# Loading the weight pieces of the projections two pieces ahead of their split, in three slots

## The chip, the cores and the metric

The kernel runs on one core of one Trainium2 chip. The metric is the device time of one execution in microseconds (us), as a median over runs.

## The reference

Two batches of 2048 tokens with 2048 channels are normalised; the result goes through one head of attention (width 512) and through a gated low-rank branch, and both are added to the input.

```python
def attn(x, Wqkv, bqkv, Wo, bo):            # d = 512
    q, k, v = split3(einsum('bsc,cf->bsf', x, Wqkv) + bqkv)
    attn = softmax(einsum('bqd,bkd->bqk', q, k) / sqrt(d))
    return einsum('bqd,dc->bqc', einsum('bqk,bkd->bqd', attn, v), Wo) + bo

def ffn(x, A_w, B_w, Wq_w, keys):           # 64 experts of rank 8, top 16
    scores = einsum('bsr,er->bse', einsum('bsd,rd->bsr', x, Wq_w), keys)
    gate = softmax_of_top16_scattered(scores)
    z = einsum('bsd,nd->bsn', x, A_w)       # n = 64 * 8 = 512
    return einsum('bsn,on->bso', z * repeat(gate, 8), B_w) * 2

x = x + attn(layernorm(x), ...) + ffn(layernorm(x), ...)
```

## The kernel before

All products keep single-precision quality by splitting each operand into a high and a low half in the type `fp32r` and multiplying three times (`product`, line 135 of the profile: low by high, high by low, high by high). The high half is a copy on ScalarE (`split_hi`, line 127), the low half a subtraction on VectorE (`split_lo`, line 130).

The work has three parts. The projections take the first 1297 us: for eight blocks of 512 tokens they make queries, keys, values, the router's inputs and the low-rank features. The attention follows, then the output projection. Blocks are taken in pairs, and in the projections a pair's four quarter products (two token blocks by two halves of the channels, two halves of the features) are replaced by seven products of sums and differences, named `P1` to `P7`. The sums of weights are made once, during the first pair, on GpSimd (`four_sums`, lines 541 to 544) and stored in device memory (`sq_d`, `sv_d`), from where the later phases load them.

The weights come in **pieces** of 128 partitions by 1024 or 1056 elements (512 or 528 KB). `pieces` lists all 218 in the order of use:

- 12 pieces `F` (block 0, features), 8 pieces `Q` and `R` (block 1, values by half of the channels), 6 pieces `P3` and 24 pieces of `P6`, `P5`, `P7`, `P4` for the rest of the first pair;
- 56 pieces for each of the other three pairs: per phase six pieces of features and two of values (`V`).

`fetch(n)` loads piece `n` on SyncE's queue (SP, line 622) and splits it. The slots are:

- a loaded piece goes into the ring `r_pw` of three slots (tags G8, G9, G7); the `F` pieces of features 0 and 2 go into the rings `r_set`, since their weights are summed in place later;
- the halves go into `r_ph`, six slots, which is three pieces' worth.

The product of piece `n` is followed by `fetch(n + 2)`, so that two pieces' halves stand ready or are being made. `features`, `values_by_half`, `third` and `phase` are the four loops over pieces; each does for one piece the product, the fetch, `flush()` (the stores that are pending), the eviction, and then a few **steps** of other work: loads of the next tokens (`x_steps`, line 640, with their normalisation, lines 647 and 648), splits of the next moving operand (`split_steps`, tile `t`), sums of weights with their loads and stores (`set_load`, line 1149; `set_out`, line 1156; `part_load`, line 1169; `part_out`, line 1178), the router's top 16 (`choose`, lines 480 to 493), and, in the last pair, key and query steps (lines 1002 to 1128).

The kernel is written with a framework that traces the calls and lets a planner set the order on each engine's queue: an instruction takes a place when, in the plan, its inputs and its slot are there, and of several the one called first goes first. Semaphores follow from the order of the calls. `behind(...)` adds edges to this: what is called in the block is queued, on each engine, behind the last instruction recorded under the names given. The steps stand behind `"sp"`, and `last["sp"]` is the newest weight load.

Of the kernel before, what the change touches and what calls it, by code (L numbers as in the profile page):

```python
# [8 lines left out]
F32 = mybir.dt.float32  # L9
FR = mybir.dt.float32r  # L10
# [52 lines left out]
def attn_ffn_kernel(ctx: ExitStack, tc, x, xT, wq, wv, wob, bqk, bv, bo, keysT, out):  # L63
# [20 lines left out]
    def wide(*js):  # L84
        return Ring(sb, *(f"G{j}" for j in js))
# [40 lines left out]
    def split_hi(hi, src):  # L126
        return nc.scalar.copy(hi, src)  # L127

    def split_lo(lo, src, hi, eng=None):
        return (eng or nc.vector).tensor_tensor(lo, src, raw(hi), ALU.subtract)  # L130
# [61 lines left out]
    r_ph = wide(0, 1, 2, 3, 4, 5)  # L192
# [126 lines left out]
    def first_block(steps):  # L319
# [128 lines left out]
        for c2 in range(N2):  # L448
            w = wv_piece(1, c2)
            if c2 == N2 - 1:  # L450
                fetch(0)
            for t in range(NT):
                mul(ps[t], w, t, c2)
            with behind("sp", "pe", "dve"):
                for st in steps[c2 : c2 + 1] if c2 + 1 < N2 else steps[c2:]:
                    st()
        fetch(1)
        for t in range(NT):
            values_out(0, t, 1, r_ev, qr, ps[t])
# [95 lines left out]
    def value_sums(m):  # L555
# [33 lines left out]
    pieces = [  # L589
        (0, "F", 2 * p + f1, ch) for p in range(NFP // 2) for ch in range(2) for f1 in range(2)  # L590
    ]
# [8 lines left out]

    r_set = {0: big(*GROUPS[0]), 2: big(*T_SLOTS[8:])}

    def fetch(n):

        if n >= len(pieces):
            return
        j, ph, it, g = pieces[n]
        w = WHERE.get(ph)
        ring = r_pw
        if ph == "F":  # L610
            shape, src = [P, HC * P], wq[0, g][it]
            ring = r_set.get(it, r_pw)
        elif ph in ("Q", "R"):
            shape, src = [P, HC // 2, VH], wv[it, int(ph == "R")][:, 4 * g : 4 * g + 4, :]
        elif it == "V":
            shape = [P, HC // 2, VH]
            src = sv_d[w][g] if isinstance(w, int) else wv[w][:, 4 * g : 4 * g + 4, :]
        else:
            shape = [P, HC * P]
            src = sq_d[w][it] if isinstance(w, int) else wq[w][it]  # L620
        ws = ring(shape, F32, "pw")
        last["sp"] = nc.sync.dma_start(ws, src)
        if ph == "F" and it in r_set:
            held[it, 0, g] = ws
        hi, lo = (r_ph(shape, FR, "pw") for a in range(2))
        last["hi"] = split_hi(hi, ws)
        last["dve"] = split_lo(lo, ws, hi)
        ready[n] = hi, lo
# [178 lines left out]
    def phase(j, ph, n, more={}):  # L807
# [9 lines left out]
        for m, it in enumerate(items):  # L817
# [4 lines left out]
            for g in range(2 if it == "V" else 1):  # L822
                w = ready.pop(n)
                n += 1
                if it != "V":
                    for c in range(HC):
                        product(
                            ps, lambda a: w[a][:, c * P : (c + 1) * P],
                            lambda b: ops[c // 2][b][:, c % 2, :], c == 0, c == HC - 1,
                        )  # L830
                else:
                    for cc in range(HC // 2):
                        c = g * HC // 2 + cc
                        for t in range(NT):
                            sl = slice(t * P, (t + 1) * P)
                            product(
                                ps[t][:, :VH], lambda a: ops[c // 2][a][:, c % 2, sl],
                                lambda b: w[b][:, cc, :], c == 0, c == HC - 1,
                            )
                fetch(n + 1)  # L840
# [26 lines left out]
    def features():  # L867


        tiles, qT, wk, gx = {}, None, None, {}  # L870
        for k, (_, _, fp, ch) in enumerate(pieces[:12]):
            if ch == 0:
                tiles[fp] = acc()
            ps, w = tiles[fp], ready.pop(k)
            if fp >= 2 * 2 and ch == 0:
                gx[fp - 4] = gate(gfs[0], fp - 4)
            for c in range(HC):
                product(
                    ps, lambda a: w[a][:, c * P : (c + 1) * P], lambda b: xn[ch * HC + c][b],
                    c == 0 and ch == 0, c == HC - 1, ch == 1,  # L880
                )
            last["dve1"] = last["dve"]
            fetch(k + 2)
            flush()
            if ch == 0:
                if fp % 2 == 0:
                    XU[0, fp // 2] = r_xu([P, 2, T], F32, "xu")
                nc.scalar.copy(XU[0, fp // 2][:, fp % 2, :], ps)
            else:
                feature_out(0, ND * (fp // 2) + fp % 2, ps, gx)  # L890
            with behind("pe"):
                if k == 0:
                    qT = router(qr)
                if k == 1:
                    wk = choose(qT)
                if k == 4:
                    gfs[0] = gates(0, wk)
            with behind("sp", "pe", "dve1"):
                for st in beside_F.get(k, []):
                    st()  # L900
        return len(tiles) * 2

    def values_by_half(n):

        for ph in "QR":
            tiles = [tsp[0, ph, 0], tsp[0, ph, 1]]
            for h in range(2):
                ps = [acc() for t in range(NT)]
                for g in range(2):
                    w = ready.pop(n)  # L910
                    n += 1
                    for cc in range(HC // 2):
                        c = g * HC // 2 + cc
                        x_ = tsp[0, ph, c // 2]
                        for t in range(NT):
                            sl = slice(t * P, (t + 1) * P)
                            product(
                                ps[t][:, :VH], lambda a: x_[a][:, c % 2, sl],
                                lambda b: w[b][:, cc, :], c == 0, c == HC - 1,
                            )  # L920
                    last["dve1"] = last["dve"]
                    fetch(n + 1)
                    if g == 1:
                        flush()
                        values_half_out(ph, h, ps)
                        flush()
                    with behind("sp", "pe", "dve1"):
                        for st in beside_V.get((ph, h, g), []):
                            st()
        return n  # L930
# [20 lines left out]
    def third(n):  # L951

        r_w = big(25), big(27), big(28)
        for m, it in enumerate(MIXED):
            ps, w = acc(), ready.pop(n)
            n += 1
            for c in range(HC):
                product(
                    ps, lambda a: w[a][:, c * P : (c + 1) * P],
                    lambda b: tsp[0, "R", c // 2][b][:, c % 2, :], c == 0, c == HC - 1,  # L960
                )
            last["dve1"] = last["dve"]
            fetch(n + 1)
            flush()
            if it % 2 == 0:
                WU[it // 2] = r_w[it // 2]([P, 2, T], F32, "wu")
            nc.scalar.copy(WU[it // 2][:, it % 2, :], ps)
            with behind("sp", "pe", "dve1"):
                for st in beside_V.get(m, []):
                    st()  # L970
        return n
# [257 lines left out]
    n = features()  # L1229
    qr1 = const.tile([P, NT, 32], F32, name="qr1", bufs=1)  # L1230
    nc.gpsimd.memset(qr1, 0.0)
    n = values_by_half(n)
    r_t = big(*T_SLOTS[4:], *T_SLOTS[:4])
    n = third(n)
# [3 lines left out]
    n = phase(0, "P6", n, {0: [la], 1: [sa, one], 3: [oa], 4: [lb]})  # L1238
    n = phase(0, "P5", n, {0: [sb_], 2: [ob], 3: [lc]})
    n = phase(0, "P7", n, {0: [sc_], 2: [oc], 3: [ld]})  # L1240
    n = phase(0, "P4", n, {0: [sd_], 2: [od]})
    for j in PAIRS[1:]:
        for ph in PHASES:
# [5 lines left out]
            n = phase(j, ph, n)  # L1249
# [16 lines left out]
    r_ph = wide(0, 1, 2)  # L1266
# [477 lines left out]
    for g in range(begin[-1]):  # L1744
# [6 lines left out]
        j, n = divmod(g, NG1)  # L1751
# [131 lines left out]
```

## Time and profile before

| | |
|---|---|
| runs, us | 2580.57, 2581.15, 2585.92; median 2581.15 |
| span of the profiled execution, us | 2582.2 (the page gives no other time of this execution) |
| granted TensorE clock, mean | 0.998 |
| TensorE (PE) busy | 2556.8 us |
| VectorE (DVE), ScalarE (ACT), GpSimd (POOL) busy | 1981.2, 926.9, 560.8 us |
| DMA | 615.41 MB, mean 238 GB/s |
| weight pieces: ScalarE high half, `pw<-pw` | 218 of 1058 ns |
| weight pieces: VectorE low half, `pw<-pw` | 218 of 1324 ns |
| weight pieces: load, issue to landing | 3.2 / 3.8 / 8.7 us (least, median, most) |

PE is the matrix engine's multiplication and PEld its weight load. SPq marks an instruction of SyncE's queue, mostly the issue of a DMA. A timeline line has the start, the duration, the engine, the line of the kernel, the operation, output and input tiles, and in brackets how long the engine was idle before it and what ended that. A line of the view of waits has who waited for whom, the total in us, the number of times and the longest.

### The profile page before, as it was taken

What the parts mean: (1) busy time and instruction counts of PE and PEld (TensorE: products, weight loads), DVE (VectorE), ACT (ScalarE), POOL (GpSimd) and SP (SyncE); (2) the same over time, 40 slices, a digit from 0 to 9 for tenths busy, and PEclk for the clock granted to TensorE, in tenths of its full rate; (3) what the DMA queues carried; (4) which work ended last, traced back from release to release, by engine and by line L of the source; (5) the groups of instructions that cost most, each with busy time, mean ns of one, the idle gap of its engine ahead of it and who ended that gap; (6) DMA issues with size and microseconds to landing.
All of it is one profiled execution on the core that took longest, in us unless ns stands there. A gap on an engine that the chain in (4) does not pass through costs nothing. (4 is left out here: it accounts for less than half of the span.)

```text
span 2582.2 us, 34227 instructions
## 1 busy us (share of the span) xinstructions
PE 2556.8 (99%) x12546; PEld 2159.7 (84%) x12546; DVE 1981.2 (77%) x2692; ACT 926.9 (36%) x1327; POOL 560.8 (22%) x340
## 2 busy tenths in 40 slices
PE   9999999999999999999999999999999999999999
PEld 8897888888888889888887878878878888888887
DVE  7788997867778678777668768688597777797675
ACT  4333333232332323343345446354364222332221
POOL 2382310001000000000000000000013565576654
PEclk9999999999999999999999999999999999999999
DMA  8988964668356673678899798898897554665552
GB/s 297 311 300 276 354 224 144 227 212 274 125 176 225 211 250 120 201 269 270 315 310 309 240 338 278 282 324 290 277 320 265 182 162 157 203 200 179 167 168 101
DMA packets 334297, 615.41 MB, mean 238 GB/s; under 512 B 28409, under 2 KB 151345, under 8 KB 334129
## 3 DMA queue, kind: packets, MB, share of 16 engines
q1 hardware_dynamic: 318864, 583.33, 67.2%
q10 hardware_dynamic: 15264, 29.89, 3.3%
q8 instruction: 99, 1.62, 0.3%
q14 instruction: 70, 0.57, 0.1%
HBM read 457.76 MB, written 155.35 MB: 237 GB/s over the span
## 5 line engine op out<-in xcount | busy, mean ns | idle before, releaser
L135 PE MATMUL acc<-t,pw 128*128 128x512 f32 x3744 | 859.0, 390 | 6.4 <-DVE t L130 4.7
L135 PEld LDWEIGHTS acc<-t,pw 128*128 128x128 f32 x3744 | 699.8, 188 | 153.9 <-DVE t L130 6.4
L1629 PE MATMUL acc<-wb,s 128*128 128x512 f32 x2688 | 609.6, 389 | 0.0
L1629 PEld LDWEIGHTS acc<-wb,s 128*128 128x128 f32 x2688 | 504.4, 188 | 105.0 <-DVE s L130 0.2
L1613 POOL TENSOR_TENSOR xo<-xo,bo_bc 128x512 f32<-128x512 f32 x128 | 213.5, 1675 | 884.5 <-DMA bo_bc<-in_bo 592.3
L127 ACT CAST pw<-pw 128x1024 fp32r<-128x1024 f32 (+1 forms) x218 | 230.5, 1058 | 442.1 <-PE acc L135 287.8
L135 PE MATMUL acc<-ph,vt 128*128 128x512 f32 x1536 | 376.7, 390 | 0.3 <-ACT ot L1474 0.2
L130 DVE TENSOR_TENSOR pw<-pw 128x1024 fp32r<-128x1024 f32 (+1 forms) x218 | 288.7, 1324 | 95.9 <-ACT pw L127 94.3
L135 PEld LDWEIGHTS acc<-ph,vt 128*128 128x128 f32 x1536 | 287.7, 188 | 62.1 <-issue 1.2
L1335 PE MATMUL acc<-qt,kt 128*128 128x512 f32 x1344 | 333.9, 390 | 2.6 <-ACT sp L1345 1.5
L1335 PEld LDWEIGHTS acc<-qt,kt 128*128 128x128 f32 x1344 | 250.9, 188 | 58.9 <-DVE qt L130 2.2
L135 PE MATMUL acc<-pw,t 128*128 128x264 f32 x2400 | 295.9, 285 | 2.9 <-DVE pw L130 0.9
L135 PEld LDWEIGHTS acc<-pw,t 128*128 128x128 f32 x2400 | 294.2, 189 | 5.3 <-ACT pw L127 1.1
L127 ACT CAST s<-xz 128x1024 fp32r<-128x1024 f32 x112 | 118.0, 1054 | 375.1 <-PE acc L1629 300.3
L130 DVE TENSOR_TENSOR s<-xz,s 128x1024 fp32r<-128x1024 f32 x112 | 177.8, 1589 | 41.0 <-ACT s L127 41.0
L130 DVE TENSOR_TENSOR t<-xq,t 128x1024 fp32r<-128x1024 f32 x108 | 141.9, 1321 | 24.3 <-ACT t L127 24.1
L535 POOL TENSOR_TENSOR zt<-zt,g 128x512 f32<-128x512 f32 x28 | 44.6, 1603 | 516.0 <-DMA g<-gd 274.6
L127 ACT CAST t<-xq 128x1024 fp32r<-128x1024 f32 x108 | 113.1, 1051 | 114.1 <-DVE xq L667 59.6
L1618 DVE TENSOR_TENSOR xo<-xo,acc 128x512 f32<-128x512 f32 x128 | 86.9, 680 | 52.1 <-POOL xo L1659 25.2
L127 ACT CAST ph<-sp 128x512 fp32r<-128x512 f32 x128 | 79.4, 620 | 109.4 <-PE acc L135 108.5
L1654 POOL TENSOR_TENSOR xo<-xo,u 128x512 f32<-128x512 f32 x64 | 111.5, 1772 | 21.5 <-DVE u L1652 21.4
L225 DVE BATCH_NORM_STATS2 st<-xs 128x6 f32<-128x512 f32 x128 | 85.0, 683 | 39.5 <-DMA xs<-in_x 39.2
(174 smaller groups left out, 2229.4 us busy)
## 6 DMA issues: line engine op xcount, KB each, us to landing
vt<-v_d SPq DMA_DIRECT2D x128, 512.0 KB, 5.4
kt<-kp_d SPq DMA_DIRECT2D x224, 256.0 KB, 5.7
pw<-sq_d SPq DMA_DIRECT2D x96, 512.0 KB, 4.3
pw<-in_wq SPq DMA_DIRECT2D x72, 512.0 KB, 3.7
xo<-in_x SPq DMA_DIRECT2D x128, 256.0 KB, 3.0
xz<-oz_d SPq DMA_DIRECT2D x64, 512.0 KB, 4.4
out_y<-xo SPq DMA_DIRECT2D x128, 256.0 KB, 2.6
xq<-in_xT SPq DMA_DIRECT2D x56, 512.0 KB, 5.1
```

Of the source, the lines that this page charges most:

```text
L127: return nc.scalar.copy(hi, src)
L130: return (eng or nc.vector).tensor_tensor(lo, src, raw(hi), ALU.subtract)
L135: last["pe"] = nc.tensor.matmul(ps, st(a_), mv(b_), start=first and n == 0, stop=end and n == 2, skip_group_check=more,)
L225: nc.vector.bn_stats(st[:, parts, :], xt[:, h * 512 : (h + 1) * 512])
L535: nc.gpsimd.tensor_tensor(zt, zt, gx[n], ALU.mult)
L1335: last["pe"] = nc.tensor.matmul(ps, st[:, d, a, :], mv[c][:, d, :], start=not more and d == 0 and i == 0, stop=d == 1 and i == 2, skip_gro ...
L1613: nc.gpsimd.tensor_tensor(xs, xs, bo_bc[q // (NB // 2 * NH), c], ALU.add)
L1618: nc.vector.tensor_tensor(xs, xs, ps, op)
L1629: nc.tensor.matmul(ps, st[a_][:, kk, sl], mv[b_], start=not more and kk == 0 and n == 0, stop=kk == ND - 1 and n == 2, skip_group_check=more,)
L1654: nc.gpsimd.tensor_tensor(xo[q, t, a, 1], xo[q, t, a, 1], v, ALU.add)
```

## The change

`fetch` is divided. `load_piece(n)` takes the slot and issues the load of piece `n`, once; `fetch(n)` now calls it for `n` and for `n + 1` before it splits piece `n`. The slots, the number of loads and of splits, and the places where `fetch` is called stay as they are.

```diff
+    loaded = {}
+
+    def load_piece(n):
+
+        if n >= len(pieces) or n in loaded:
+            return
...
-        ws = ring(shape, F32, "pw")
+        ws = loaded[n] = ring(shape, F32, "pw")
         last["sp"] = nc.sync.dma_start(ws, src)
         if ph == "F" and it in r_set:
             held[it, 0, g] = ws
-        hi, lo = (r_ph(shape, FR, "pw") for a in range(2))
+
+    def fetch(n):
+
+        if n >= len(pieces):
+            return
+        load_piece(n)
+        load_piece(n + 1)
+        ws = loaded[n]
+        hi, lo = (r_ph(ws.shape, FR, "pw") for a in range(2))
         last["hi"] = split_hi(hi, ws)
         last["dve"] = split_lo(lo, ws, hi)
         ready[n] = hi, lo
```

More of the change, by code (lines that the diff above doesn't have):

```diff
@@ L601, in attn_ffn_kernel @@
     r_set = {0: big(*GROUPS[0]), 2: big(*T_SLOTS[8:])}
-    def fetch(n):
-        if n >= len(pieces):
+    loaded = {}
+    def load_piece(n):
+        if n >= len(pieces) or n in loaded:
             return
```

## The prediction

> **What bounds the kernel now.** I read the page's busy shares first, then PE's waits, then the timelines round each of them.
>
> The page's first lines:
>
> ```profile
> span 2582.2 us, 34227 instructions
> ...
> PE 2556.8 (99%) x12546; PEld 2159.7 (84%) x12546; DVE 1981.2 (77%) x2692; ACT 926.9 (36%) x1327; POOL 560.8 (22%) x340
> ```
>
> PE works for all but 2582.2 - 2556.8 = 25.4 us. The change adds and removes no matmul, so 25.4 us is all that any reordering could win, and only the part that lies in the projections (up to about 1297 us) is in its reach. The view of waits for PE, window 140 to 1300 us (total, times, longest):
>
> ```profile
> PE acc L135 <- DVE t L130: 5.3, 5, 2.4
> PE acc L135 <- DVE pw L130: 2.6, 2, 1.7
> PE acc L135 <- ACT pw L127: 0.9, 1, 0.9
> PE acc L135 <- ACT yv L941: 0.5, 1, 0.5
> ```
>
> Together 9.3 us. Only 3.5 us (2.6 + 0.9) name a weight piece (`pw`); 5.3 us name the moving operand `t`. PE's timeline shows where the larger ones are:
>
> ```profile
> 170.89 8.99 PE L135 MATMUL acc<-pw,t 128*128 128x264 f32 x72 [0.66 <-DVE t L130]
> 204.32 19.60 PE L135 MATMUL acc<-t,pw 128*128 128x512 f32 x85 [1.72 <-DVE pw L130]
> 226.32 1.65 PE L135 MATMUL acc<-t,pw 128*128 128x512 f32 x6 [2.40 <-DVE t L130]
> 228.59 6.87 PE L135 MATMUL acc<-t,pw 128*128 128x512 f32 x29 [0.61 <-DVE t L130]
> 1288.31 0.39 PE L135 MATMUL acc<-pw,t 128*128 128x264 f32 x1 [0.90 <-ACT pw L127]
> 1289.60 7.54 PE L135 MATMUL acc<-pw,t 128*128 128x264 f32 x47 [0.90 <-DVE pw L130]
> ```
>
> **Where a load really stands.** The code calls a load just before its split. The queue does not keep to that. One piece in the steady part, timeline round 726 us:
>
> ```profile
> 725.15 1.05 ACT L127 CAST pw<-pw 128x1024 fp32r<-128x1024 f32 x1 [0.21 <-PE acc L135]
> 726.24 1.23 DVE L130 TENSOR_TENSOR pw<-pw 128x1024 fp32r<-128x1024 f32 x1 [0.63 <-ACT pw L127]
> 727.49 0.33 SPq L622 DMA_DIRECT2D pw<-in_wq  x1
> ```
>
> The low half ends at 726.24 + 1.23 = 727.47, and a load is issued 0.02 us later: the split has just freed one of three slots, and the load that takes it is that of the piece three further on. Its own split comes some 14 us later, and a load lands in 3.8 us (median of the tile's view). The planner has moved the load as far ahead as three slots allow, one step further than the change asks. Counting loads and splits through the trace, most of the 206 pieces from the 13th on go like this. There the change can move nothing: 0 us: some 10 us lie between landing and split, and a load that lost one product of 5.5 us would still be in time.
>
> The exceptions are two crowded stretches of SP's queue, 115 to 205 us (weight sums) and 1196 to 1281 us (key and query steps). There a load is issued up to 15 us after its slot is free, in the order in which the code calls it, and its split waits for it:
>
> ```profile
> 188.45 1.05 ACT L127 CAST pw<-pw 128x1024 fp32r<-128x1024 f32 x1 [4.15 <-DMA pw<-sq_d]
> 194.89 1.05 ACT L127 CAST pw<-pw 128x1024 fp32r<-128x1024 f32 x1 [1.62 <-DMA pw<-sq_d]
> ...
> 1272.80 0.42 SPq L622 DMA_DIRECT2D pw<-in_wv  x1
> 1280.33 0.49 SPq L622 DMA_DIRECT2D pw<-in_wv  x1
> 1287.18 1.07 ACT L127 CAST pw<-pw 128x1056 fp32r<-128x1056 f32 x1 [8.21 <-DMA pw<-in_wv]
> ```
>
> **The change, part by part.** No instruction, byte or slot is added. Each load is called one piece earlier, so in a crowded stretch it takes about the place of the load before it.
>
> *The last piece (1280.33).* It takes the place of the one at 1272.80, 7.5 us sooner. It landed at about 1287.1 (6.8 us after issue), so now at about 1279.6; high and low half (1.07 + 1.26 us) are done by 1282 to 1283, before PE wants them at 1287.4. Both waits of 0.90 us go: -1.80 us. Nothing else is late there, since `kt` and `qt` loads are queued behind this load already.
>
> *The piece at 204.32.* Its load moves from 188.10 to the place of 185.36 or before, 2.7 us or more, and the high half (194.89, 1.62 us after ACT fell idle for the landing) moves with it. The low half, at 203.05, did not wait for it: it stood on DVE behind the top-k work of `choose` (197.6 to 203). Whether it gets ahead of that is up to the planner: 0 to -1.72 us. I take -1.72, since its high half is ready before that work starts; the 0 stays in the range.
>
> *The operand waits (`t`, 5.3 us).* These splits have no load in them. I take 0; the gain rival below prices them.
>
> *What is queued behind.* `behind("sp", ...)` puts a product's other steps behind the newest load, which is now one piece further and can start only when the split three before it is done. The trace shows that this binds early on:
>
> ```profile
> 67.94 0.34 SPq L622 DMA_DIRECT2D pw<-in_wq  x1
> 68.34 2.58 SPq L1149 DMA_DIRECT2D wu<-in_wq  x2
> ...
> 78.21 2.78 DVE L130 TENSOR_TENSOR pw<-pw 128x1024 fp32r<-128x1024 f32 x1 [6.34 <-ACT pw L127]
> ...
> 117.14 2.00 ACT L127 CAST t<-xq 128x1024 fp32r<-128x1024 f32 x2
> ...
> 122.30 2.35 DVE L130 TENSOR_TENSOR t<-xq,t 128x1024 fp32r<-128x1024 f32 x2
> ```
>
> `set_load(2)` (`wu`) left directly behind piece 7's load. Now it stands behind piece 8's, whose slot is freed by the split that ends at 78.21 + 2.78 = 80.99: 13 us later. What waits for it is POOL's sums, whose last waited until 100.99 for another split anyway: covered. The next place is `set_out(2)`, stores at 111.25 to 117.1. It now stands behind piece 12's load, whose slot is freed at 116.7 (DVE low half at 115.49, 1.21 us). That is 5.5 us for the first store, about 2 for the last. These stores free the slots of the first `Q` splits of `t` (117.14 on ACT, 122.30 on DVE). With 4 us to land, DVE's pair moves to about 125, 2.7 us later. The DVE chain behind it ended at 134.0, and the product that needs it starts at 137.0: 3.0 us of cover, so 0. If the shift persists to the `t` split at 170.85, which is already 0.66 us late, it costs up to 2.7. Against that DVE waits 9.1 us for high halves of `pw` between 140 and 215 (two waits, the tile's view), and these shrink. I take 0 and keep 0 to +2.7.
>
> [...]
>
> **Sum.** -1.80 - 1.72 = -3.5 us. The profiled execution's span, 2582.2 us (the page gives no other time of its own), becomes 2578.7. It stands 1.05 us above the runs' median of 2581.15, so on the median the forecast is 2577.6. Its own range: nothing from the piece at 204 and +2.7 from `t` give 2582.1; another 2 us from `t` waits give 2575.6.
>
> **The rivals.** About 0.2% (5.2 us) is what a measurement of this kernel can tell from no change: below 2576.0 is faster, above 2586.3 slower.
>
> *DVE catches up (faster).* If the 9.1 us in which DVE waited for high halves go, DVE comes earlier to its `t` splits, and the 2.40 + 0.61 us at 226 to 229 vanish with the 3.5: 2574.6. With everything in the projections gone, 9.3 us: 2571.8. For it: DVE is 83% busy from 140 to 235 us (78.92 of 95), so a few us of slack matter. Against: the split before 226.32 also stands among statistics that wait for `xs` loads. 0.27.
>
> *The steps queued behind a later load delay DVE (slower).* The place is 111 to 230 us: the stores of `set_out(2)` wait for a slot, then `t`, then DVE, in order. The small shift of 2.7 us, passed on to 170.9 and again to 226, both without slack, costs 5.4; less the 1.80 won at the end that is 2584.8, still "same". The whole 5.5 us of the first store passed on to both places costs 11.0, less 3.0 of cover and the 1.80: 6.2, or 2587.4. With another 2.7 at the piece of 204, 8.9: 2590. It decides once DVE's chain slips by more than the 3.0 us of cover at 137 and again behind it. For it: DVE is nearly without pause from 83 to 139. Against: the loads that DVE waits for come earlier in the same stretch. 0.28.
>
> *Nothing happens.* The queue already has all loads as early as slots allow, and the crowded ones are reordered without effect: 2581 to 2582. This is inside "same" with the forecast.
>
> **How the numbers follow.** The forecast has 0.30 and "nothing happens" 0.15, together 0.45 for the same; DVE catching up 0.27, DVE delayed 0.28. The range 2572 to 2590 goes from all projection waits gone to the price of the slower rival; I leave out about 0.04 below and 0.15 above, since a planned order that shifts can lose more than it can win.
>
> **What would show it.** Right: the two waits at 1288 gone, the last `pw` load some 7 us earlier; loads at 188 to 200 us earlier, ACT's waits of 4.15 and 1.62 us smaller; in the steady part a load still 0.0 us after the low half that frees its slot; PE's waits from 140 to 1300 us about 6 us in all instead of 9.3. Wrong: PE waiting for `t` between 137 and 230 us for longer than 5 us, `wu` loads not moved from 68 to 81, or new PE waits in the attention part.

## The result, and the profile after

The changed kernel takes 2587.93 us (median of 14 runs, 2583.05 to 2591.39) where the kernel before, run beside it, takes 2583.03 (14 runs, 2580.17 to 2585.98): ratio 1.0018, interval 1.0012 to 1.0025. It is 4.9 us slower, small but clear of no change. A second comparison (experiment 18) gave 2587.26 against 2582.33, ratio 1.0018 (1.0009 to 1.0027). The forecast was 2577.6. The one profiled execution of experiment 13 ran at a granted clock of 0.76 and is left out of everything below.

The page of the changed kernel begins:

```profile
span 2586.9 us, 34208 instructions
...
PE 2559.1 (99%) x12546; PEld 2162.5 (84%) x12546; DVE 1983.2 (77%) x2692; ACT 928.8 (36%) x1327; POOL 564.4 (22%) x340
```

The span is 4.7 us longer. PE does the same 12546 matmuls in 2.3 us more (2559.1 against 2556.8) and is idle for 2.4 us more (27.8 against 25.4). So two things are to be explained: longer waits, and matmuls that run slower. The view of waits for PE, 140 to 1300 us (total, times, longest), and PE's timeline where they are:

```profile
PE acc L135 <- DVE t L130: 5.7, 2, 5.1
PE acc L135 <- DVE pw L130: 5.7, 2, 4.3
```

```profile
170.19 9.00 PE L135 MATMUL acc<-pw,t 128*128 128x264 f32 x72 [0.60 <-DVE t L130]
200.82 19.29 PE L135 MATMUL acc<-t,pw 128*128 128x512 f32 x72 [4.33 <-DVE pw L130]
221.47 16.62 PE L135 MATMUL acc<-t,pw 128*128 128x512 f32 x72 [1.35 <-DVE pw L130]
268.14 20.64 PE L135 MATMUL acc<-t,pw 128*128 128x512 f32 x83 [5.10 <-DVE t L130]
...
1303.08 7.14 PE L1345 MATMUL acc<-qt,kt 128*128 128x512 f32 x30 [0.65 <-DVE vs L302]
```

In all 11.4 us instead of 9.3, and in other places: 4.33 and 1.35 at 200 and 221 us for weight pieces (1.72 before), nothing at 226 (3.01 before), 5.10 at 268 (1.45 before), nothing at 1288 (1.80 before). Following the start of the same matmul through both executions (times of the kernel before), the changed kernel is 0.7 us ahead at 194 us, 7.8 behind at 267, 7.3 behind at 1200, 4.4 behind at 1315 and 4.7 behind at the end. The whole loss is made between 194 and 268 us, in the first pair; 900 us of projections behind it change by half a microsecond, and some 3 us come back behind 1280.

**Slower matmuls.** The windows view (stretch, its length, then each engine's busy time and count, the granted clock, DMA share, GB/s) of the stretches behind the two long waits:

```profile
199.70:206.50 6.80, 5.68 (x13) 4.46 (x14) 6.80 (x30) 2.45 (x6) 3.49 (x2) 0.50 0.71 247
206.50:209.90 3.40, 3.40 (x16) 2.78 (x15) 3.40 (x7) 0.61 (x2) 0.00 (x0) 1.00 0.95 282
...
268.00:271.40 3.40, 3.26 (x8) 2.58 (x9) 3.40 (x5) 0.00 (x0) 0.00 (x0) 0.50 0.02 8
271.40:274.80 3.40, 3.40 (x17) 2.76 (x16) 3.28 (x6) 1.05 (x1) 0.00 (x0) 1.00 0.58 166
```

Behind each long wait PE is granted half its clock (0.50), for 6.8 and for 3.4 us: 8 matmuls where the next stretch has 17. Experiments 7 and 8 ask what that costs.

**Where the first pair went wrong.** The load that the prediction followed, `set_load(2)` (`wu`), is where it was foreseen, behind the ninth load of a piece:

```profile
67.82 0.34 SPq L624 DMA_DIRECT2D pw<-in_wq  x1
...
79.22 0.34 SPq L624 DMA_DIRECT2D pw<-in_wq  x1
...
80.08 0.90 SPq L1159 DMA_DIRECT2D wu<-in_wq  x2
```

It left at 68.34 before. What was not foreseen is what it does to POOL. The last of the sums that need it, in POOL's and DVE's timelines, before:

```profile
100.99 4.40 POOL L544 TENSOR_TENSOR pw<-pw 128x1024 f32<-128x1024 f32 x1 [11.10 <-DVE pw L130]
...
101.92 1.21 DVE L130 TENSOR_TENSOR pw<-pw 128x1024 fp32r<-128x1024 f32 x1
106.30 1.43 DVE L130 TENSOR_TENSOR pw<-pw 128x1024 fp32r<-128x1024 f32 x1 [3.17 <-ACT pw L127]
```

and after:

```profile
104.76 15.75 POOL L544 TENSOR_TENSOR pw<-pw 128x1024 f32<-128x1024 f32 x1 [7.30 <-DVE pw L130]
...
105.69 2.35 DVE L130 TENSOR_TENSOR pw<-pw 128x1024 fp32r<-128x1024 f32 x2
107.96 2.35 DVE L657 TENSOR_TENSOR xq<-xq,mb 128x1024 f32<-128x1024 f32 x2
110.23 2.35 DVE L658 TENSOR_TENSOR xq<-xq,mb 128x1024 f32<-128x1024 f32 x2
112.50 1.22 DVE L130 TENSOR_TENSOR pw<-pw 128x1024 fp32r<-128x1024 f32 x1
113.63 2.35 DVE L657 TENSOR_TENSOR xq<-xq,mb 128x1024 f32<-128x1024 f32 x2
115.90 2.35 DVE L658 TENSOR_TENSOR xq<-xq,mb 128x1024 f32<-128x1024 f32 x2
118.36 3.24 DVE L130 TENSOR_TENSOR pw<-pw 128x1024 fp32r<-128x1024 f32 x1
```

Each time the sum ends 2.26 us after DVE's first pause: before, DVE stops at 101.92 + 1.21 = 103.13 and the sum ends at 105.39; after, DVE works without a gap until 115.90 + 2.35 = 118.25 and the sum ends at 120.51. One sum, begun 3.8 us later, ends 15.1 us later, and in between DVE had no pause. In ten profiled executions (the kernel before, the changed kernel, experiments 1 to 7 and 18) the sum ends 2.25 to 2.28 us after the end of the unbroken run of DVE's in which it began, be it of 2 instructions or of 12; in experiment 12 it ran after the first instruction of such a run, before the next, and took 3.23 us. All sums of weights stand behind it on POOL: the first `part_sums` start at 120.5 instead of 105.4, the last at 197.1 instead of 184.9. Their loads and stores share SP's queue with the weight pieces, and so the piece for 200 us is late, not early:

```profile
189.48 2.27 SPq L1179 DMA_DIRECT2D hs<-in_wq  x4
191.79 0.43 SPq L624 DMA_DIRECT2D pw<-sq_d  x1
...
198.26 1.04 ACT L127 CAST pw<-pw 128x1024 fp32r<-128x1024 f32 x1 [2.33 <-DMA pw<-sq_d]
...
199.11 0.43 DVE L302 TENSOR_TENSOR vs<-acc,yv 128x264 f32<-128x264 f32 x1 [4.27 <-DMA v_d<-vs]
199.46 1.31 DVE L130 TENSOR_TENSOR pw<-pw 128x1024 fp32r<-128x1024 f32 x1
```

This piece (the third of the mixed pass `P3`) was issued at 185.36 before; now four loads of the sum chain (`hs`) are in front of it. It has landed when its high half starts, at 198.26, and PE waits until its low half is done.

### The profile page after: what moved, and what is told of

The parts are those of the page before. It is cut to its first block, busy times and chain, and to the rows that moved or that the text cites. A ratio compares the mean times of both kernels' runs of the same rounds, so it can differ in the third digit from the quotient of the medians.

```text
span 2586.9 us, 34208 instructions
## 1 busy us (share of the span) xinstructions
PE 2559.1 (99%) x12546; PEld 2162.5 (84%) x12546; DVE 1983.2 (77%) x2692; ACT 928.8 (36%) x1327; POOL 564.4 (22%) x340
## 3 DMA queue, kind: packets, MB, share of 16 engines
q8 instruction: 99, 1.62, 0.3%
## 5 line engine op out<-in xcount | busy, mean ns | idle before, releaser
L1623 POOL TENSOR_TENSOR xo<-xo,bo_bc 128x512 f32<-128x512 f32 x128 | 207.6, 1629 | 886.8 <-DMA bo_bc<-in_bo 587.1
L130 DVE TENSOR_TENSOR s<-xz,s 128x1024 fp32r<-128x1024 f32 x112 | 170.5, 1523 | 46.4 <-ACT s L127 46.4
```

Of the source, the lines that this page charges most:

```text
L1623: nc.gpsimd.tensor_tensor(xs, xs, bo_bc[q // (NB // 2 * NH), c], ALU.add)
```

## The experiments

Two theories stood at the start. **T1, the pins:** the steps that `behind("sp")` puts behind the newest load now wait for a later slot; that delays the sum chain. **T2, the call order:** the loads called earlier stand in front of other transfers, whatever the pins. A third, T3: any other order of the plan costs or wins some us by chance. All kernels but one (experiment 4, 5 runs) were timed 10 to 12 times beside 26 to 35 runs of the kernel before; single runs of one kernel spread by about 2.3 us (standard deviation), so a ratio's interval is about 0.09% to each side, and the time of one profiled execution says less than its waits. The kernel before had medians of 2581.81 to 2583.45 beside them, so rows are compared by their ratios.

| | loads one further ahead for | steps stand behind | median, us | ratio to before (interval) |
|---|---|---|---|---|
| 1 | all | own load | 2583.73 | 1.0004 (0.9995 to 1.0013) |
| 2 | 196 and up | newest | 2583.68 | 1.0003 (0.9994 to 1.0012) |
| 3 | below 26 | newest | 2583.56 | 1.0004 (0.9995 to 1.0013) |
| 4 | below 12 | newest | 2591.21 | 1.0037 (1.0024 to 1.0050) |
| 5 | all | own below 12, then newest | 2586.22 | 1.0016 (1.0007 to 1.0025) |
| 6 | 26 and up | newest | 2580.88 | 0.9994 (0.9986 to 1.0003) |
| 7 | all, fill | newest | 2587.40 | 1.0019 (1.0010 to 1.0028) |
| 8 | 196 and up, fill | newest | 2583.45 | 1.0011 (1.0002 to 1.0020) |
| 9 | 26 and up | own load | 2581.18 | 0.9993 (0.9984 to 1.0002) |
| 10 | 26 and up | newest, value sums own | 2580.57 | 0.9990 (0.9980 to 1.0000) |
| 11 | none, second value sums late | | 2585.62 | 1.0010 (1.0002 to 1.0019) |
| 12 | none, `set_load(2)` late | | 2588.57 | 1.0019 (1.0011 to 1.0028) |
| 13 | 26 and up | newest, second value sums own | 2582.26 | 0.9998 (0.9988 to 1.0009) |
| 14 | none, first value sums late | | 2581.50 | 0.9998 (0.9990 to 1.0007) |
| 15 | all but 12 to 19 | own load | 2582.32 | 1.0003 (0.9994 to 1.0012) |
| 16 | as 13 | as 13 | 2582.71 | 1.0007 (0.9998 to 1.0016) |
| 17 | as 10 | as 10 | 2582.28 | 1.0000 (0.9991 to 1.0008) |
| 18 | the changed kernel | | 2587.26 | 1.0018 (1.0009 to 1.0027) |

PE's waits by place, in the profiled execution of each (us), and how many of the two splits of `t` at each place took 2.1 us or more instead of 1.2:

| | 190 to 223, `pw` | 222 to 237, `t` | slow splits | 255 to 271, `t` | slow splits |
|---|---|---|---|---|---|
| before | 1.72 | 3.01 | 2 | 1.45 | 0 |
| changed | 5.68 | 0 | 0 | 5.10 | 1 |
| changed again (18) | 5.52 | 0 | 0 | 2.25 | 2 |
| 1 | 4.33 | 3.14 | 2 | 0 | 0 |
| 2 | 2.61 | 2.22 | 2 | 1.77 | 0 |
| 3 | 5.52 | 0 | 0 | 0.84 | 0 |
| 4 | 5.61 | 2.88 | 2 | 0 | 0 |
| 5 | 3.41 | 0 | 0 | 4.30 | 2 |
| 6 | 2.42 | 0 | 0 | 4.47 | 2 |
| 7 | 4.30 | 0 | 0 | 3.12 | 2 |
| 8 | 0.56 | 2.30 | 2 | 0 | 0 |
| 9 | 2.70 | 2.91 | 1 | 0.73 | 0 |
| 10 | 1.62 | 3.10 | 1 | 0.43 | 0 |
| 11 | 2.61 | 5.01 | 2 | 0 | 0 |
| 12 | 1.72 | 4.81 | 2 | 0 | 0 |
| 14 | 1.98 | 0 | 0 | 1.19 | 0 |
| 15 | 2.42 | 1.62 | 1 | 0.93 | 0 |
| 16 | 2.19 | 0 | 0 | 3.37 | 2 |
| 17 | 1.73 | 1.83 | 1 | 1.14 | 0 |

### Pins or call order: experiments 1, 4, 5, 3

*1.* The pins restored, the loads ahead:

```diff
...
-        last["sp"] = nc.sync.dma_start(ws, src)
+        issued[n] = nc.sync.dma_start(ws, src)
...
         load_piece(n + 1)
+        last["sp"] = issued[n]
```

> The loads are called two pieces ahead as in the changed kernel, but the steps that stand behind the newest weight load stand behind the load of the piece that is being split, as before the change. Theory T1 (the pins: steps of the first pair that stand behind the newest load now wait for a later slot, which delays the sum chain and with it the splits at 200 and 268 us): the loss of 7.8 us between 194 and 267 us is gone, and the gain at 1288 us (2.97 us) stays: 2577 to 2581 us against 2583 for the kernel before; PE's wait at 200 us is back at 2 us or less. Rival T2 (the call order: transfers of the sum chain stand behind loads that are called earlier, whatever the pins): still 2586 to 2589 us, with PE's wait at 200 us of 4 us. Rival T3 (any other order of the plan costs or wins some us by chance): neither; the two stretches get other waits.

Measured: the loss is gone (1.0004). But the wait at 200 us is not back at 2 us; it is 4.33, and the gain at the end is not to be seen in the time (2583.73, not 2577 to 2581). T1 holds for the time as a whole, T2 for one wait.

*4.* The loads ahead in the first pass alone (`if n + 1 < 12: load_piece(n + 1)`):

> A load is called one piece further ahead only for pieces below 12, the very first pass, in which the steps of the sum chain stand behind the loads. T1: most of the loss is here, since these steps are pinned in this pass: 2587 to 2591 us, PE's wait at 200 us of 3 us or more. T2 (the loads at 185 to 205 us stand wrong in the queue because pieces 13 to 25 are called earlier): no loss, 2582.5 to 2584 us, PE's wait at 200 to 204 us of 1.7 us as before the change.

Measured: 2591.21, the largest loss of all, with the twelve pieces that are used before 140 us. POOL's sum shows the same 15.76 us. The long waits come only behind that pass: 2.3 us between 161 and 165, 5.61 at 201, 2.88 at 236.

*5.* Only the first pass' pins restored (`last["sp"] = issued[n if n < 12 else min(n + 1, len(pieces) - 1)]`):

> The changed kernel, but during the first pass (pieces below 12) the steps that stand behind the newest load stand behind the load of the piece being split, as before the change; from piece 12 on they stand behind the newest load, as changed. T1 in its narrower form (each pin counts where it stands): the first sums of the chain start at 105 us again (120.5 in the changed kernel, 104.9 with all pins restored), the last at 191 us or before (197.1), and the wait at 200 us is then 4.3 us or less; the wait at 268 us (5.10 us in the changed kernel, none with all pins restored) belongs to pins in the later passes and stays at 4 to 5 us: 2584 to 2587 us. If the first pass' pins set everything that follows: no wait over 2 us at 268 us, 2582 to 2584.5 us. T2 (call order alone): the last sums start at 196 us or later, 2586 to 2589 us. T3: waits of over 2 us at other places than 200, 229 and 268 us.

Measured: POOL's sum is as it was,

```profile
100.84 4.40 POOL L544 TENSOR_TENSOR pw<-pw 128x1024 f32<-128x1024 f32 x1 [11.10 <-DMA hs<-in_wq]
```

the chain's last sums start at 190.1, the wait at 200 us is 3.41, and the wait behind 260 us stays, 4.30: the narrower form of T1. The time is in the range given for it. But it is hardly better than the changed kernel's (1.0016 against 1.0018), and above experiment 1's (1.0004), though these two intervals meet: restoring the first pass' pins alone does not win the loss back.

*3.* The loads ahead below piece 26 only:

> A load is called one piece further ahead only for pieces below 26, the first pair's beginning. T1 and T2 alike: the whole loss is here and no gain: the slip stands at +7 to +8 us behind 267 us, 2590 to 2591 us in the end. T3: the slip is not the +7.8 us of the changed kernel, or the pieces behind 26 shift it again.

A miss for both theories: 1.0004, not 2590. The waits at 200 and 220 us are the changed kernel's (5.52), but the wait at 226 us is gone and the one at 268 has not come. So the two halves of the change (3 and 6) cost nothing each by their medians (their intervals reach up to 3.4 and 0.8 us), and together 4.9 us. The next groups show part of why. Experiment 3 also has the changed kernel's late sums, the 15.75 us on POOL and the last `part_sums` at 196.4: by themselves they do not make the loss. And it is faster than 4, which has fewer loads ahead; the profile of 4 has another 2.88 us at 236, where the first value sums met the splits of `t`, and that of 3 has not, but why the loads of pieces 12 to 25 win so much back was not run.

*12.* The suspected cost alone, in the kernel before:

```diff
-        5: [lambda: set_load(2), lambda: set_out(0)],
-        6: [lambda: set_sums(2)] + x11[0] + [L[0]],
+        5: [lambda: set_out(0)],
+        6: [lambda: set_load(2), lambda: set_sums(2)] + x11[0] + [L[0]],
```

> The kernel before, with one thing moved: the load of the first pass' second set of weights for the sums stands one step later (beside product 6, just ahead of these sums, instead of beside product 5). Theory: the first sums on POOL start 10 us or more later (105 us before, 120.5 in the changed kernel), the later sums follow, the last ones end at 196 us or later instead of 190, and PE's waits between 160 and 240 us grow as with the loads called ahead in the first pass alone (2591): 2586 to 2592 us. Rival (the first pass' pins do no harm by themselves, the chain catches up): the last sums end by 192 us, 2581.5 to 2583.5 us.

Measured: 2588.57, in the range given, with no load of a piece moved. The path is partly another: the first `part_sums` start at 109.9, not at 115 or later, the last end at 195.7, and PE waits 2.00 us at 107, 2.17 at 168 and 4.81 at 234. That a sum load one step later costs some 5 us by itself is shown; that it must pass through the 15.75 us is not.

### The wait at 262 to 268 us: experiments 6, 9, 10, 11, 13, 14, 16, 17

*6.* The loads ahead from piece 26 on:

> A load is called one piece further ahead only from piece 26 on, so that the first pass, the values and the mixed passes up to 205 us are the kernel before. Theory T1 with pins in the later passes: the wait of 1.4 to 2.3 us at 204 us stays, the wait at 262 us (1.45 us before, 5.10 us in the changed kernel, 0.84 us with the change below piece 26 alone) grows to 4 or 5 us, the waits at 1288 us go: 2582 to 2585 us. If the wait at 268 us needs the late sum chain of the first pass as well: no more than 2 us there, and 2579.5 to 2582 us. T3: a new wait of over 2 us somewhere between 270 and 1280 us.

Measured: 4.24 us at 262 (4.47 with a second wait), as T1 had it; the wait needs no late sum chain. But the wait at 226 us (3.01 before) is gone, and the time is not longer (2580.88, below T1's range). The timelines of DVE and POOL tell what both waits are. Before, at 226 (`x2`: two splits in one line):

```profile
223.28 1.90 POOL L541 TENSOR_TENSOR ws<-ws 128x528 f32<-128x528 f32 x1 [33.05 <-DMA ws<-in_wv]
225.26 2.19 POOL L542 TENSOR_TENSOR ws<-ws 128x528 f32<-128x528 f32 x1
...
223.95 4.58 DVE L130 TENSOR_TENSOR t<-xq,t 128x1024 fp32r<-128x1024 f32 x2
```

and in experiment 6, at 262:

```profile
258.37 2.16 POOL L543 TENSOR_TENSOR ws<-ws 128x528 f32<-128x528 f32 x1
260.61 2.18 POOL L544 TENSOR_TENSOR ws<-ws 128x528 f32<-128x528 f32 x1
...
259.30 4.57 DVE L130 TENSOR_TENSOR t<-xq,t 128x1024 fp32r<-128x1024 f32 x2
```

POOL's groups of value sums (`ws`) are also steps behind `"sp"`. One load later, the first group comes after the splits of `t` for `P6` (POOL 226 to 234, splits at 222 to 224) and the second moves from 247 to 254 us to 254 to 263, onto the splits for `P5`. Beside a sum of POOL's a split took 2.3 us instead of 1.2 (the pairs above 4.58 and 4.57 us, the pair at 260.59 in the kernel before, with no sum beside it, 2.35). In the table no row has slow splits at both places; where there are none at 226 PE does not wait there, and where there are none at 262 the wait there is under 1.8 us. (In the changed kernel's own profile only one of the two is slow; the rest of its 5.10 us is the statistics' load ahead of them, for which DVE waits 2.71 us instead of 1.62.)

*9.* All pins restored, loads ahead from 26:

> The loads one piece further ahead from piece 26 on, and the steps that stand behind the newest load kept behind the load of the piece being split, as before the change, all through. Theory (the wait at 262 us is made by the second value sums: pinned one load later, POOL does them from 254 to 263 us beside DVE's two splits of t, which then take 2.3 us each instead of 1.2): POOL is done by 257 us, the two splits take 1.2 us each, PE's wait there is 1.8 us or less instead of 4.24, and the run is 1.5 to 4 us faster than the same without the pins (2580.9): 2577 to 2579.5 us. Rival (the wait comes from the loads called ahead in these passes, not from the pins): still 3.5 us or more of wait, 2580 to 2582 us.

*10.* Only the value sums' pins restored:

```diff
             for st in more.get(m, []):
-                with behind("sp", "pe"):
+                with behind("own", "pe"):
```

> The loads one piece further ahead from piece 26 on; only the value sums of the first pair's passes (their loads, sums and stores) are kept behind the load of the piece being split, all other steps stand behind the newest load. Theory as for the run with all pins restored: if it is the value sums alone, POOL's second group ends by 257 us, the two splits of t at 259 us take 1.2 us each, PE's wait there is 1.8 us or less: 2577 to 2579.5 us. If other pinned steps make it (the loads of the statistics and of the inputs): the splits take 1.2 us but start late, a wait of 3 us or more, 2580 to 2582 us.

Both: waits of 0.73 and 0.43 us at 262, as the theory said, with POOL done at 254.2 and 252.9:

```profile
251.52 1.33 POOL L544 TENSOR_TENSOR ws<-ws 128x528 f32<-128x528 f32 x1
...
258.89 2.35 DVE L130 TENSOR_TENSOR t<-xq,t 128x1024 fp32r<-128x1024 f32 x2
```

It is the value sums alone. The times did not follow as expected (2581.18 and 2580.57, not 2577 to 2579.5): the wait at 226 came back (2.91 and 3.10), so some 4 us at one place were only exchanged for 3 at the other.

*11.* The collision made by hand, in the kernel before (the second group's load at item 5 of `P6` instead of 4):

> The kernel before, with one thing moved: the load of the second group of value sums stands one step later in pass P6 (beside its sixth item instead of its fifth), with all loads of weight pieces as they were. Theory: this alone makes the wait at 262 us: POOL's second group runs at 255 to 263 us, the two splits of t take 2.3 us each, PE's wait there is 3.5 to 4.5 us instead of 1.45, 2 to 5 us longer: 2584 to 2587 us. Rival (the collision needs the loads called ahead): the wait stays at 1.4 to 2 us, 2581.5 to 2583.5 us.

Measured 2585.62, as the theory's sum, but at another place:

```profile
230.10 10.11 PE L135 MATMUL acc<-t,pw 128*128 128x512 f32 x32 [5.01 <-DVE t L130]
```

The second group ran from 256.2 to 261.7 and the splits came only at 264.5, behind it, at 1.2 us each. The 5 us at 230 are the first group's collision, with statistics that waited 4.17 us for their load ahead of it. So this run does not show what it was made for.

*14.* The first group one item later, in the kernel before; *13* and *16* keep both groups away with the loads ahead (`behind("sp" if ph == "P6" and m < 4 else "own", "pe")`); *17* repeats 10:

> The kernel before, with the first group of value sums one item of pass P6 later (loads beside the second item, sums beside the third), and all weight loads as they were. Theory: POOL begins at 226 us or later, the two splits of t take 1.2 us each, the waits of 2.4 and 0.6 us at 226 and 229 us are gone and the wait at 262 us stays at 1.5 us or less: 2 to 3 us faster than the kernel before, 2579.5 to 2581 us. Rival: the wait moves to 262 us, where the second group, behind the first on POOL, now meets the next splits: 2582.5 to 2585 us.

> The loads one piece further ahead from piece 26 on; of the value sums the first group stands behind the newest load (one load later than before the change, so that POOL begins it at 226 us, behind DVE's two splits of t) and the second behind the load of the piece being split (as before, done by 254 us, ahead of DVE's next two splits of t). Theory (collision of POOL's sums with DVE's splits): all four splits of t take 1.2 us, no wait of over 0.8 us at 222 to 230 us nor at 260 to 264 us; 3 us less than the run with all sums as before the change (2580.6): 2576.5 to 2579 us. Rival (lateness of the loads or of the statistics): the splits take 1.2 us, but PE still waits 2 us or more at one of the two places: 2579.5 to 2582 us.

> The kernel with the first group of value sums behind the newest load and the second behind the load of the piece being split, once more, for a profile at full clock. Theory (collision): the four splits of t at 222 to 230 and 258 to 264 us take 1.2 us each, PE's waits there are 0.8 us or less; the time by its first comparison 2580 to 2584 us. Rival: a wait of 2 us or more stays at one of the two places although the splits take 1.2 us.

> The kernel with the loads ahead from piece 26 on and the value sums held as before the change, once more. If it is faster than the kernel before (first comparison 2.6 us, 0.999 with an interval up to 1.000): 2579 to 2581 us, interval below 1.000. If the first comparison was luck: 2581.5 to 2583.5 us.

In 14 all four splits take 1.2 us, and PE's waits there are 0 and 1.19 us, as the theory says:

```profile
204.28 29.11 PE L135 MATMUL acc<-t,pw 128*128 128x512 f32 x120 [1.98 <-DVE pw L130]
259.54 10.74 PE L135 MATMUL acc<-t,pw 128*128 128x512 f32 x46 [1.19 <-DVE t L130]
```

The profiled execution has a span of 2576.7 us, but the median of eleven is 2581.50, and the interval reaches from 2.6 us faster to 1.8 us slower: the 2 to 3 us expected are not decided. 13 has 2582.26 us, above both its ranges. In 16 the second group did not go back to 254 us (POOL 254.1 to 262.2) and collided again, 3.37 us: the edit did not do what it was made for. In 17 the gain of 10 was not repeated (1.0000). No version here is shown to beat the kernel before.

### The wait at 200 us with the pins restored: experiment 15

As 1, but the values' pieces 12 to 19 not ahead:

> All pins as before the change, the loads one piece further ahead except for pieces 12 to 19, the first pair's values. With all of them ahead and the pins restored PE waited 4.33 us at 200 us, and the second sums of the chain began at 135.5 us (128.8 before). Theory A (the loads of the values' pieces, called ahead, stand in front of the chain's own loads): the second sums begin at 130 us or before, the wait at 200 to 204 us is 2.3 us or less: 2579 to 2582.5 us. Theory B (the loads of pieces 20 to 25, called ahead, stand in front of the chain's last transfers): still 3 us or more at 200 us, 2582.5 to 2585 us.

Measured: the second sums start at 129.1 us (135.5 in 1, 128.8 before), the wait is 2.42 us (4.33 in 1). This is theory A but for a tenth. With all loads ahead, the load of a values' piece, which still waits for its slot, stands on SP in front of the chain's own transfers. In 1 SP issues nothing from 111.3 us until the low half at 115.06 has freed the slot, and the other stores of `set_out(2)` follow the load:

```profile
115.06 1.21 DVE L130 TENSOR_TENSOR pw<-pw 128x1024 fp32r<-128x1024 f32 x1
116.30 0.33 SPq L624 DMA_DIRECT2D pw<-in_wv  x1
116.68 0.43 SPq L1167 DMA_DIRECT2D sq_d<-pw  x1
```

In 15 the first store of `pw` leaves at 111.45 (111.73 in the kernel before), and the loads of the next sums (`hs`) at 121.52 instead of 128.06. So T2 is real; its price, about 2 us of wait, is that of one execution each.

### The end of the projections: experiment 2

> A load is called one piece further ahead only for pieces 196 and up, the last pair's last passes; everything up to 1190 us is then the kernel before. T1 and T2 alike: the two waits of 0.90 us and the half clock of 3.4 us at 1288 us are gone, so 2579 to 2580.5 us against 2583 (2.4 to 3 us faster). T3, or the later stages giving it back (the slip grew again by 1.6 us behind 1390 us in the changed kernel): 2581.5 to 2584 us.

Measured 1.0003: no gain. The waits at 1288 us are gone, here and in the other 12 executions with the last loads ahead. But they are not a fixed 1.80 us in the others: of six executions with the last loads as before, the kernel's own has 1.80, the others 0, 1.41, 0.82, 1.45 and 0, 0.91 us in the mean. And with the loads ahead PE then waits a little later for the last values, 0.92 us in the mean of the 13. Experiment 9:

```profile
1296.24 3.94 PE L1347 MATMUL acc<-qt,kt 128*128 128x512 f32 x16 [1.39 <-DVE vs L302]
```

Between 1200 and 1315 us the 13 executions with the loads ahead win 2.58 us in the mean on the kernel before's profile, the six without 2.09 (from 0, its own, to 3.94): by the means the change is worth about 0.5 us there, which this spread does not tell from nothing, and the profile of before was an unlucky one.

### What the half clock costs: experiments 7 and 8

*7.* The changed kernel with 14 matmuls of no use ahead of the product at 200 us. *8.* Experiment 2 with 17 such matmuls in the waits at 204, 226 and 262 us.

```diff
+            if m == 2:
+                x_ = tsp[0, "R", 0][0]
+                fill(ps, x_[:, 0, :P], x_[:, 0, :], 14)
             for c in range(HC):
                 product(
```

> The changed kernel with 14 products more, of no use to the result, that PE does while it waits at 200 us: they write into the accumulator that piece 22's own first product then starts afresh. About 0.23 us each, 3.2 us of the wait of 4.33 us, so PE is idle for 1.1 us there. Theory on the clock: the half clock of 6.8 us behind this wait (granted 0.50) is brought by the idle time and not by the work; it is gone, and 2.5 to 3 us with it: 2584.5 to 2585.5 us against 2588. Rival (the half clock is due to something else, such as power or the DMA load): it stays at 200 us, 2587.5 to 2588.5 us.

> The loads one piece further ahead from piece 196 on only, and products of no use in three waits of the kernel before: 6 ahead of the first product of piece 23 (wait at 204 us, 1.7 to 2.3 us), 6 ahead of the first of pass P6 (226 us, 1.6 to 2.4 us), 5 ahead of the first of pass P5 (262 us, 1.45 to 1.8 us), 1.2 to 1.4 us each. If the idle time of a window brings the half clock and the late loads end the waits at 1288 us: no half clock between 30 and 1380 us, 2579 to 2581.5 us against 2583. If the fill only moves the waits: 2582.5 to 2585 us.

In 7 the half clock at 200 us goes with the idle time. The wait is 0.97 us (4.33 in the changed kernel), and the stretch that had 0.50 has 1.00:

```profile
199.70:206.50 6.80, 5.83 (x25) 4.43 (x24) 6.80 (x30) 2.35 (x5) 3.52 (x2) 1.00 0.73 257
...
221.50:224.90 3.40, 3.40 (x10) 2.64 (x9) 3.12 (x5) 2.40 (x3) 0.00 (x0) 0.51 0.97 289
```

In 8 there is none between 30 and 1380 us (mean granted clock 0.999; 0.998 in the kernel before, which has one of 3.41 us at 1290). But neither is faster: 7 has 1.0019 where the changed kernel has 1.0018, and 8 has 1.0011 where experiment 2 has 1.0003. In 7, PE is 2.0 us earlier than in the changed kernel from 210 to 220 us, then waits 2.88 us at 221 (1.35 there), with the half clock behind it (0.51), and is 1.2 us later. By this profile SP's queue and DVE set the end from 190 to 225 us, and PE's slow matmuls filled time that it would have waited anyway. The theory of where the half clock comes from stands for the wait at 200 us; the price of 2.5 to 3 us that I gave it was not found, though the intervals leave room for 2 us.

### Once more the changed kernel: experiment 18

> The changed kernel itself once more, for a second profile. If the waits belong to the order of the work: PE waits 3 us or more at 200 us and 2.5 us or more at 266 to 268 us again, with both splits of t there beside POOL's sums (one at least at 2.3 us), half clock behind at least one of them, and no wait at 1288 us; 2586 to 2589 us. If they belong to one execution: one of the two waits is under 1.5 us.

Measured: 3.37 us at 201 and 2.15 at 222 with half clock behind both (72 matmuls in 18.25 and 18.23 us, where the first execution has 16.62 behind its 1.35 us at 221); 2.25 in all at 267 to 269 (2.5 was the bound), both splits there at 2.3 us; none at 1288; and 1.97 at 172, where the first execution has 0.60. POOL's sum is the same to 0.01 us:

```profile
104.83 15.75 POOL L544 TENSOR_TENSOR pw<-pw 128x1024 f32<-128x1024 f32 x1 [7.30 <-DVE pw L130]
```

The waits belong to the order of the work; their sizes differ by up to 3 us from one execution to the next.

## Why the prediction was wrong, point by point

- *The steady part, 0 us.* Right. A load still leaves when the low half frees its slot (734.04 + 1.23 = 735.27, issue at 735.29), and the distance to the kernel before stays at 7.8 to 7.3 us from 300 to 1200 us:

```profile
734.04 1.23 DVE L130 TENSOR_TENSOR pw<-pw 128x1024 fp32r<-128x1024 f32 x1 [0.63 <-ACT pw L127]
...
735.29 0.33 SPq L624 DMA_DIRECT2D pw<-in_wq  x1
```

- *What is queued behind: 0.* **This is the step that failed first.** The move of `wu` was right (12 us for the 13 foreseen). "Covered" was not: I compared it with the time at which POOL's last sum began, 100.99, and took for granted that the sum then runs. It begins 3.8 us later and ends 15.1 us later, 2.26 us after DVE's first pause at 118.25. That a later `set_load(2)` loses by itself experiment 12 shows (+5.1 us by the medians); 4, with the first pass' loads alone ahead, loses 8.6. In the changed kernel the term as a whole is wrong, by experiment 1 (all pins restored, no loss); the first pass' share of it is open, since restoring that pass alone leaves 1.0016 (5). The second place, `set_out(2)`, came out at 0 by luck: its first store left 6.3 us later (117.57 for 111.25), and DVE's pair of splits not 2.7 but 8.6 us later (130.93 for 122.30), far more than the 3.0 us of cover; PE had no wait at 137 all the same, and 0.60 at 170 (0.66 before).
- *"It takes about the place of the load before it."* Wrong in the first pair, the premise of the -1.72: the loads at 185.36 and 188.10 went to 191.79 and 193.55, behind the delayed `hs` loads, and PE's wait of 1.72 us for the second of these pieces became one of 4.33 for the first.
- *The operand waits `t`: 0.* Wrong at both ends. The 3.01 us at 226 went, which the gain rival had, for another reason (it had DVE catching up; it was the value sums moving off), and 5.10 came at 268, which nobody had. I read the pins of the first pass and not those of `P6` and `P5`, which hold POOL's value sums; experiments 6, 9 and 10 show that these make the wait at 262.
- *The last piece: -1.80.* The waits went, and the load moved, by 5.5 us on the kernel's own time. The term is mis-sized: about -0.5 by the means of experiment 2's section, and not clear of 0, since the 1.80 was one execution's draw and "nothing else is late there" left out the last values.
- *No term for DVE beside POOL.* The sum has none, and the runs show one in both directions: splits of `t` of 2.3 us instead of 1.2, and POOL's sum of 15.75 us, where the four sums of that shape that start at 69 to 88 us of the kernel before took 2.39 to 2.44. The kernel before has it elsewhere too: the low half's median is 1.97 us from 140 to 215 us, where POOL sums weights, and 1.23 us from 700 to 1180. In the changed kernel a run of 12 instructions of DVE's with no gap between them lies beside the long sum, while in 107 to 115 us of the kernel before, where DVE's work has no gap either, several sums ended and both engines were slower (DVE's pairs at lines 647 and 648 took 4.54 and 3.44 us instead of 2.35, POOL's sums of 128x512 2.15 instead of 1.3). Why the sum did not end so at 105 us is open.
- *No term for the clock.* Of the span's growth of 4.7 us 2.3 are PE's busy time, and behind the two long waits 10.2 us were granted 0.50. In experiments 7 and 8 no loss of its own is seen.
- *The slower rival*, 2587.4 at 0.28, had the right cause, the steps behind a later load, and by chance the size. Its path was another (stores of `set_out(2)`, then `t` at 170.9 and 226); the wait of over 5 us for `t` came, at 268 and not between 137 and 230.

That the pins cost the time is shown (experiment 1); by which path is in part argued. How the halves add up to more than their sum is answered, as far as it is, by the two collisions. Each half alone moves the first value sums off the splits at 226 (-3 us); together they do it once, and the costs at 200 and at 262 to 268 us are paid both. That is argued from the table of waits, not run by itself, and the waits of one execution order the kernels only roughly: the three columns add up to 6.18 us before and to 10.78 and 7.77 in the two executions of the changed kernel, but to 4.97 in experiment 15 and 4.70 in 17, which are no faster than before. So T3 is not excluded for a part of the loss.

## What to carry to other kernels

A change of a queue's order is costed by what it makes late, not by what it makes early: list every step that is tied to the moved instruction, and for each ask which engine it lands beside. Cover has to be counted to the end of the covering work, under the load that the engines have then. Where single runs spread by 2 us, a wait of 1 to 2 us in one profile is no term of a sum; look whether a second execution of the same code has it.

## What the runs showed that was not expected

- *Which waits had a half clock behind them.* In the changed kernel's trace the granted clock switches at 199.70, 206.53, 267.97, 271.38, 1394.37 and 1397.78 us, all multiples of 3.41 us apart; in the kernel before at 1290.09 and 1293.50. With the executions divided into such stretches of 3.41 us, ten between 60 and 1300 us have 1.1 us or more of PE's idle time. Behind three of them the next one is at 0.50: 1.80 us of idle time in the kernel before (from 1286.67 us), 3.21 and 3.41 in the changed one (from 196.29 and 264.56). Behind a fourth, with 1.12 us (from 199.70) and at 0.50 itself, it is 0.50 again. Behind the other six it is not: 1.72, 1.20, 1.76 and 1.45 us before (from 201.23, 221.71, 225.13 and 259.26), 1.29 and 1.52 in the changed kernel (from 220.18 and 261.14). Outside that range the wait of 1.54 us near 1388 us lies in one stretch of the kernel before, and the next is at 1.00; in the changed kernel it begins in one stretch and has 1.38 us in the following, and the next is at 0.50. So the length of a wait alone did not tell whether the half clock came.
- *What the long row is.* By my estimate, from the 2.26 us behind DVE's first pause and the 2.39 to 2.44 us of the four sums in the kernel before, POOL's 15.75 us are a sum of 2.3 us that stood for 13; the row itself does not tell the two apart.
